# Attention of layers 1 to 3: turned probabilities and values on halves of the array's rows, router and projection matmuls moved behind the values

## The chip, the cores and the metric

One core of a Trainium2 chip. The metric is the device time of one execution, in microseconds (us); the kernel before has a median of 2300.88 us over 3 runs (2300.48 to 2303.32). One further execution was taken by the profiler.

## The reference, cut to what matters

Four layers of gated cross attention, each followed by a feed-forward part, on x of 16 batches x 56 tokens x 256 features. Layer 0 is another kind of attention. In layers 1 to 3 every token has 16 heads, and each batch attends to its own 1500 context rows of 64 numbers, which are the keys and the values at once:

```python
k_r    = einsum('bld,hdr->bhlr', kv_rope, W_kr)
scores = einsum('bhsr,bhlr->bhsl', q_r, k_r)
attn   = softmax(scores, axis=-1)
ctx_c  = einsum('bhsl,bld->bhsd', attn, kv_rope)
out    = (ctx_c through w_kc_kv).reshape(b, s, H * K) @ Wo.T
x      = x + tanh(g_xattn[l]) * out
```

All is float32. The feed-forward parts are mixtures of experts in layers 0, 2 and 3 (a router picks experts token by token) and one matrix with fp8 rounding in layer 1.

## The kernel before, in words

**Tiles and steps.** The 16 batches are taken in 8 tiles of two batches. The weights of the keys are absorbed into the queries, so a query is 64 numbers long; those of a tile's two batches (b = 0 and 1) lie on partitions 0 to 63 and 64 to 127 of `qT`. A tile has 2 x 56 x 16 / 2 = 896 query columns for each batch, cut into nq = 7 steps of QT = 128. So a layer has 56 steps, and layers 1 to 3 have 168. `attention_mla` runs them in a software pipeline: in iteration k, step k gets its scores, step k-1's probabilities are turned, and step k-2's values are made. Every engine's order is the order of the program (`in_order`); the tile framework adds the semaphores.

**One iteration** on the TensorE (PE), in order:

- S, `scores` (L760): six calls, for each third z of the keys and each batch b one of 64 rows x 500 columns. A float32 call is two passes, so this is 12 matmuls. The two batches use different halves of the array's rows and different PSUM banks: `sp0[z]` for b = 0, a third of `sp1` for b = 1.
- V, `values` (L840): 24 calls, each for one of 12 chunks c of 125 keys and one b: 125 rows, 64 columns, 128 moving columns; 48 matmuls, all into one bank, `lent[0]`, taken from the two-bank pool `misc`. The two batches use different halves of the array's columns.
- T, `turned` (L822): 24 transposes of 128 queries x 125 keys in six groups n of 4, one bank per group (n = 1 to 3 use `sp0[n - 1]`, the others `misc`). A transpose is one matmul.

Around them: VectorE (DVE) makes the maxima (L772, L774, L777), copies the groups n = 0 and 1 out of PSUM (L830) and multiplies the values by the inverse denominators in `keep` (L851, two pieces of 64 x 128, or four in the step j = 3, which straddles two column blocks). ScalarE (ACT) makes the exponentials (L783, L792) and copies groups n = 2 to 5 (L832). GpSimd (POOL) adds denominators (L803, L804).

**Other matmuls in the iteration.** When a tile is finished, a generator carries its projection and the next part's preparation on, one piece per iteration at marked slots ("X", "Z", "R", "E"). The pieces with matmuls stand at slot "Z": the projection (L863), and then in layers 2 and 3 three of the router (L1022, L1032, L1073 with L1075), in layer 1 three of the fp8 matrix (L1640, L1662, L1640). Below they are called products. They write into free columns of the bank that holds the values: `room(n)` gives `lent[0][:, QT:QT + n]`. Slot "Z" lies between the second and the third group of transposes. In layer 1 the next tile's keys are also turned (`keys`, L745, three parts of 4 transposes, into a bank of their own), between S and V. In layers 2 and 3 they are loaded instead.

**The loop** that the change reorders, shortened:

```python
if val:
    val.values()
    val.keep()
for i in range(6):
    if new and i == 2:
        new.exps1()
        new.invert()
    if turn:
        turn.turned(i)
    if i == 1:
        ...
        go("Z")
    if turn:
        turn.keep_turned(i)
    if i == 1:
        go("R")
go("E")
```

Of the kernel before, what the change touches and what calls it, by code (L numbers as in the profile page):

```python
# [36 lines left out]
F32 = mybir.dt.float32  # L37
# [4 lines left out]
ALU = mybir.AluOpType  # L42
AX = mybir.AxisListType
# [6 lines left out]
NT = B // 2  # L50
KP, KC = 125, 12
DQ = 192
QT = 128
# [29 lines left out]
def flamingo_kernel(ctx: ExitStack, tc: tile.TileContext, d: dict, out: bass.AP):  # L83
    nc = tc.nc
# [9 lines left out]
    in_order = tc.keep_in_program_order  # L94

    def misc():
        return psm.tile([128, 512], F32, tag="m", name="m_ps")

    lent = [None]

    def room(n):

# [15 lines left out]
    ident = const.tile([128, 128], F32, name="ident")  # L118
    make_identity(nc, ident)
    tri = const.tile([TP, 16, 16], F32, name="tri")  # L120
    kv = const.tile([KP, NT, KC, 2, DC], F32, name="kv")
# [576 lines left out]
    def attention_mla(l, nxt, router=None, behind=None, tail=None):  # L698

        with ExitStack() as st:  # L700
# [3 lines left out]
            def keys_again(t):  # L704

                kvTs[t] = kp.tile([128, L], F32, name="kvT")
                in_order(nc.sync.dma_start(kvTs[t], turned_kv[t]))
# [4 lines left out]
            kvTs = {}  # L712
# [19 lines left out]
            ctxs = {}  # L732
            nq = 8 * TP // QT

            def keys(t, z):

                if l > 1:
                    if z == 0:
                        keys_again(t)
                    return  # L740
                if z == 0:
                    kvTs[t] = kp.tile([128, L], F32, name="kvT")
                ps = misc()
                for c in range(4):
                    in_order(nc.tensor.transpose(  # L745
                        ps[:, c * KP : (c + 1) * KP], kv[:, t, 4 * z + c].rearrange("p b e -> p (b e)"), ident[0:KP, 0:KP]
                    ))
                in_order(nc.scalar.copy(kvTs[t][:, z * 4 * KP : (z + 1) * 4 * KP], ps[:, 0 : 4 * KP]))
                if z == 2:
                    in_order(nc.sync.dma_start(turned_kv[t], kvTs[t]))  # L750

            class Step:
                def __init__(self, t, j):
                    self.t, self.j = t, j

                def scores(self, z):

                    t, j = self.t, self.j
                    for b, o in enumerate((sp0[z], sp1[:, z, :])):
                        in_order(nc.tensor.matmul(  # L760
                            o[:, 0 : 4 * KP],
                            qT[64 * b : 64 * b + 64, t, j * QT : (j + 1) * QT],
                            kvTs[t][64 * b : 64 * b + 64, z * 4 * KP : (z + 1) * 4 * KP],
                            start=True,
                            stop=True,
                        ))

                def maxima0(self, z):
                    if z == 0:
                        self.part = ap.tile([QT, 3], F32, name="part")  # L770
                        self.nm = [ap.tile([QT, 1], F32, name=f"nm{b}") for b in range(2)]
                    in_order(nc.vector.tensor_reduce(self.part[:, z : z + 1], sp0[z][:, 0 : 4 * KP], AX.X, ALU.max))  # L772
                    if z == 2:
                        in_order(nc.vector.tensor_reduce(self.nm[0], self.part, AX.X, ALU.max, negate=True))  # L774

# [3 lines left out]
                def exps0(self):  # L779
                    self.p = [ap.tile([QT, L], F32, name=f"p{b}") for b in range(2)]  # L780
                    self.den = ap.tile([QT, 4], F32, name="den")
                    for z in range(3):
                        in_order(nc.scalar.activation(  # L783
                            self.p[0][:, 4 * z * KP : 4 * (z + 1) * KP],
                            sp0[z][:, 0 : 4 * KP],
                            AF.Exp,
                            bias=self.nm[0],
                            accum_out=self.den[:, z : z + 1],
                        ))
# [20 lines left out]
                    for b in range(2):  # L810
                        in_order(nc.sync.dma_start(self.rep[64 * b : 64 * b + 64, :], through[b : b + 1, :].to_broadcast([64, QT])))

                def turned(self, n):

                    if n == 0:
                        self.pT = ap.tile([KP, KC, 2, QT], F32, name="pT", bufs=1)
                    z, b = n // 2, n % 2
                    ps = sp0[n - 1] if 1 <= n <= 3 else misc()
                    ps = ps[0:KP, :].rearrange("p (c q) -> p c q", c=4)
                    for c in range(4):  # L820
                        k = (4 * z + c) * KP
                        in_order(nc.tensor.transpose(ps[:, c, :], self.p[b][:, k : k + KP], ident))  # L822
                    self.turning = ps

                def keep_turned(self, n):

                    z, b, ps = n // 2, n % 2, self.turning
                    o = self.pT[:, 4 * z : 4 * z + 4, b, :]
                    if n < 2:
                        in_order(nc.vector.tensor_copy(o, ps))  # L830
                    else:
                        in_order(nc.scalar.copy(o, ps))  # L832

                def values(self):

                    lent[0] = misc()
                    self.pv = lent[0][:, 0:QT]
                    for c in range(KC):
                        for b in range(2):
                            in_order(nc.tensor.matmul(  # L840
                                self.pv[64 * b : 64 * b + 64, :], kv[:, self.t, c, b, :], self.pT[:, c, b, :], start=c == 0, stop=c == KC - 1
                            ))

                def keep(self):

                    for a in range(2):
                        lo, hi = max(self.j * QT, 448 * a), min((self.j + 1) * QT, 448 * (a + 1))
                        for b in range(2):
                            if lo < hi:
                                cols = slice(lo - self.j * QT, hi - self.j * QT)  # L850
                                in_order(nc.vector.tensor_tensor(  # L851
                                    ctxs[self.t][64 * a : 64 * a + 64, b, lo - 448 * a : hi - 448 * a],
                                    self.pv[64 * b : 64 * b + 64, cols],
                                    self.rep[64 * b : 64 * b + 64, cols],
                                    ALU.mult,
                                ))

            def project(t):
# [16 lines left out]
            def at(i):  # L875
                return steps[i] if 0 <= i < n else None

            for z in range(3 if l == 1 else 0):
                keys(0, z)
            after, wanted, pending = iter(()), "X", None  # L880

            def go(slot):

                nonlocal wanted
                if wanted[0] == slot:
                    wanted = next(after, "none")

            for k in range(n + 2):
                new, turn, val = at(k), at(k - 1), at(k - 2)
                if k == 1:  # L890

                    for _ in late:
                        pass
                    if l != 2:
                        nxt.stack.close()
                    occupy(10)
                if new:
                    if new.j == 0:
                        ctxs[new.t] = ap.tile([128, 2, H // 2 * S], F32, name="ctxT")
                    for z in range(3):  # L900
                        new.scores(z)
                        new.maxima0(z)
                    if new.t + 1 < NT and new.j in (2, 3, 4):
                        keys(new.t + 1, new.j - 2)
                if k == 0:
                    late = late()
                    next(late, None)
                go("X")
                if new:
                    new.exps0()  # L910
                    new.maxima1()
                if val:
                    val.values()
                    val.keep()
                for i in range(6):
                    if new and i == 2:
                        new.exps1()
                        new.invert()
                    if turn:
                        turn.turned(i)  # L920
                    if i == 1:
                        if pending:
                            for _ in after:
                                pass
                            after, wanted, pending = pending, "Z", None
                        go("Z")
                    if turn:
                        turn.keep_turned(i)
                    if i == 1:
                        go("R")  # L930
                go("E")
                if tail is not None and k > 0:
                    next(behind, None)
                    next(behind, None)
                if val and val.j == nq - 1:
                    pending = project(val.t)
# [917 lines left out]
```

## Time and profile before

| what | us |
|---|---|
| median of 3 runs | 2300.88 (2300.48 to 2303.32) |
| the profiled execution, its own time | 2298.12 |
| its span, first to last instruction | 2296.3 |
| PE busy (share of the span) | 2198.5 (96%) |
| PE weight loads busy | 1598.8 (70%) |
| DVE busy | 1562.3 (68%) |
| ACT busy | 1221.7 (53%) |
| POOL busy | 346.3 (15%) |
| layers' steps, 339 to 844: PE busy of 505.0 | 504.2 |
| layers' steps, 987 to 1484: PE busy of 497.0 | 494.3 |
| layers' steps, 1620 to 2113: PE busy of 493.0 | 487.8 |

The profiler's own time is 1.8 us longer than the span. A line of the timeline gives the start, the length, the engine, the kernel's line and how many instructions are merged in it; two lines of one engine can overlap, because a matmul's recorded length runs on past the start of the next. PEld is the loading of the weights (the stationary operand), which runs beside PE.

### The profile page before, as it was taken

Reading aid. Unit: us, or ns where it says so; the run is one execution under the profiler, and the core shown is the slowest. Engines: PE = TensorE matmul, PEld = TensorE weight load, DVE = VectorE, ACT = ScalarE, POOL = GpSimd, SP = SyncE. Lnnn points to the kernel's source line nnn. Section 1 sums busy time; section 2 is a strip of 40 time slices with the busy share of each in tenths; the row PEclk is TensorE's granted clock in tenths of the full one; section 3 lists DMA queues with packets and bytes.
Section 4 is the critical chain, followed back from the end, with each engine's and each line's share of the span. In section 5 each row is a group of like instructions: output and inputs, shape, how many; then the busy total and the mean of one; then the engine's idle time right before and its main releaser. Section 6 shows DMA issues by size and latency. Waiting matters only on the chain. (4 is left out here: it accounts for less than half of the span.)

```text
span 2296.3 us, 47100 instructions
## 1 busy us (share of the span) xinstructions
PE 2198.5 (96%) x17838; PEld 1598.8 (70%) x17846; DVE 1562.3 (68%) x3627; ACT 1221.7 (53%) x2675; POOL 346.3 (15%) x678
## 2 busy tenths in 40 slices
PE   8879999999999999999999999989999999999698
PEld 5647657777777784457777777745677777777465
DVE  5658457777777878767777777624677777777332
ACT  4313357666666653366666666514666666666132
POOL 1225600000000004410000000000001111101234
PEclk9779999999999999999999999999999999999799
DMA  9545450000000002100000000154001100000465
GB/s 273 183 136 163 141 158 23 22 22 23 16 15 22 23 23 81 57 20 22 25 24 24 25 12 23 49 206 142 20 22 31 30 30 21 27 22 18 135 196 168
DMA packets 106681, 153.48 MB, mean 67 GB/s; under 512 B 18319, under 2 KB 76696, under 8 KB 105417
## 3 DMA queue, kind: packets, MB, share of 16 engines
q1 hardware_dynamic: 97299, 131.83, 18.9%
q0 software_dynamic: 7600, 17.14, 2.3%
q8 instruction: 146, 2.39, 0.4%
q10 hardware_dynamic: 1542, 1.34, 0.2%
q14 instruction: 94, 0.77, 0.1%
HBM read 111.73 MB, written 40.48 MB: 66 GB/s over the span
## 5 line engine op out<-in xcount | busy, mean ns | idle before, releaser
L783 ACT ACTIVATE p<-s_ps,nm 128x500 f32<-128x500 f32 x504 | 335.2, 674 | 402.1 <-DVE nm L774 396.3
L840 PEld LDWEIGHTS m_ps<-pT,kv 125*64 125x64 f32 x8064 | 437.0, 137 | 112.5 <-issue 108.8
L840 PE MATMUL m_ps<-pT,kv 125*64 125x128 f32 x8064 | 478.2, 275 | 3.7 <-ACT pT L832 2.5
L772 DVE TENSOR_REDUCE part<-s_ps 128x1 f32<-128x500 f32 x504 | 341.8, 678 | 203.0 <-PE s_ps L760 200.0
L760 PE MATMUL s_ps<-kvT,qT 64*128 64x500 f32 x2016 | 471.7, 596 | 3.1 <-ACT qT L330 2.6
L760 PEld LDWEIGHTS s_ps<-kvT,qT 64*128 64x128 f32 x2016 | 182.4, 186 | 179.1 <-issue 115.6
L822 PE MATMUL m_ps<-ident,p 128*125 128x128 f32 x2016 | 292.6, 281 | 2.4 <-issue 2.4
L777 DVE TENSOR_REDUCE nm<-s_ps 128x1 f32<-128x1500 f32 x168 | 287.5, 1711 | 0.0
L822 PEld LDWEIGHTS m_ps<-ident,p 128*125 128x125 f32 x2016 | 246.2, 187 | 33.6 <-issue 28.2
L822 PE MATMUL s_ps<-ident,p 128*125 128x128 f32 x2016 | 265.3, 274 | 1.5 <-ACT p L783 1.0
L792 ACT ACTIVATE p<-s_ps,nm 128x1500 f32<-128x1500 f32 x168 | 254.5, 1515 | 4.5 <-DVE nm L777 4.4
L822 PEld LDWEIGHTS s_ps<-ident,p 128*125 128x125 f32 x2016 | 241.9, 188 | 4.0 <-ACT p L783 1.6
L832 ACT COPY pT<-s_ps 125x512 f32<-125x512 f32 x336 | 180.8, 595 | 99.7 <-PE s_ps L822 87.1
L803 POOL TENSOR_TENSOR den<-den 128x1 f32<-128x1 f32 x168 | 32.5, 193 | 1325.9 <-ACT p L783 1325.7
L832 ACT COPY pT<-m_ps 125x512 f32<-125x512 f32 x336 | 185.1, 619 | 0.0
L851 DVE TENSOR_TENSOR ctxT<-m_ps,rep 64x128 f32<-64x128 f32 (+1 forms) x384 | 104.3, 272 | 65.6 <-PE m_ps L840 52.0
L1336 PE MATMUL gu_ps<-wgu,xT 128*128 128x448 f32 (+2 forms) x344 | 138.3, 528 | 4.4 <-ACT xT L1326 4.4
L830 DVE COPY pT<-m_ps 125x512 f32<-125x512 f32 x168 | 116.2, 692 | 10.5 <-PE s_ps L822 0.5
L330 ACT COPY qT<-q_ps 64x224 f32<-64x224 f32 x124 | 69.7, 562 | 98.5 <-PE q_ps L378 67.1
L1361 POOL DMA_INDIRECT results<-y,to x78 | 92.8, 1189 | 169.3 <-ACT y L1360 116.9
L830 DVE COPY pT<-s_ps 125x512 f32<-125x512 f32 x168 | 114.4, 681 | 0.0
L1341 DVE TENSOR_TENSOR act<-gu_ps,act 128x224 f32<-128x224 f32 (+2 forms) x78 | 31.3, 401 | 120.7 <-ACT act L1340 88.8
(305 smaller groups left out, 2518.4 us busy)
## 6 DMA issues: line engine op xcount, KB each, us to landing
rows<-zero SPq DMA_DIRECT2D x16, 899.5 KB
kvT<-turned_kv SPq DMA_DIRECT2D x16, 750.0 KB
rep<-through SPq DMA_DIRECT2D x336, 32.0 KB
xrow<-rows SPq DMA_DIRECT2D x78, 128.5 KB
wgu<-in_L_wgu SPq DMA_DIRECT2D x21, 448.0 KB
wgu<-in_L_wgu SPq DMA_DIRECT2D x8, 1024.0 KB
back<-results SPq DMA_DIRECT2D x16, 448.0 KB
wq<-in_L_wq SPq DMA_DIRECT2D x24, 256.0 KB
```

The source lines that it names most:

```text
L760: in_order(nc.tensor.matmul(o[:, 0 : 4 * KP], qT[64 * b : 64 * b + 64, t, j * QT : (j + 1) * QT], kvTs[t][64 * b : 64 * b + 64, z * 4 * KP ...
L772: in_order(nc.vector.tensor_reduce(self.part[:, z : z + 1], sp0[z][:, 0 : 4 * KP], AX.X, ALU.max))
L777: in_order(nc.vector.tensor_reduce(self.nm[1], sp1[:, :, 0 : 4 * KP], AX.XY, ALU.max, negate=True))
L783: in_order(nc.scalar.activation(self.p[0][:, 4 * z * KP : 4 * (z + 1) * KP], sp0[z][:, 0 : 4 * KP], AF.Exp, bias=self.nm[0], accum_out=sel ...
L792: in_order(nc.scalar.activation(self.p[1].rearrange("p (z c) -> p z c", z=3), sp1[:, :, 0 : 4 * KP], AF.Exp, bias=self.nm[1], accum_out=se ...
L822: in_order(nc.tensor.transpose(ps[:, c, :], self.p[b][:, k : k + KP], ident))
L830: in_order(nc.vector.tensor_copy(o, ps))
L832: in_order(nc.scalar.copy(o, ps))
L840: in_order(nc.tensor.matmul(self.pv[64 * b : 64 * b + 64, :], kv[:, self.t, c, b, :], self.pT[:, c, b, :], start=c == 0, stop=c == KC - 1))
L851: in_order(nc.vector.tensor_tensor(ctxs[self.t][64 * a : 64 * a + 64, b, lo - 448 * a : hi - 448 * a], self.pv[64 * b : 64 * b + 64, cols] ...
L1336: in_order(nc.tensor.matmul(ps[:, s, 0:n], xT[:, k, :], wgu[:, k, s * n : (s + 1) * n], start=k == 0, stop=k == 1))
L1361: i = nc.gpsimd.indirect_dma_start(flat, bass.IndirectOffsetOnAxis(ap=to[:, 0:1], axis=0), y, None, bounds_check=B * S * top - 1, oob_is_e ...
```

## The change

Five things, all in `attention_mla`:

- The transposes work on halves of the rows: a block of 128 queries x 125 keys is two transposes of 64 queries, one on array rows 0 to 63, one on rows 64 to 127, each with 64 moving columns, into two banks. There are 48 of them, in three groups n of 16; each group fills a pair of banks.
- The banks `sp0` rotate: step k's third z lies in `sp0[(k + z) % 3]`. With a, b, c the banks of z = 0, 1, 2 of the new step, group 0 takes (a, b), group 1 (c, a `misc` bank), group 2 (a again, a `misc` bank).
- The values work on halves of the rows: 48 calls, of 64 or 61 rows, 64 columns and 128 moving columns. Rows 0 to 63 of each chunk sum into `lent[0]`, rows 64 to 124 into a second bank, `beside[0]`. `keep` multiplies each part by the inverse denominators on DVE (128 x 128, two of them), and POOL adds the two parts.
- Slots "Z" and "R" now stand right behind V and `keep`, ahead of the transposes.
- Layer 1's keys are turned in four parts of three, in the steps j = 2 to 5, behind slot "Z", into `beside[0]`.

DVE copies both halves of group 0, ACT both halves of groups 1 and 2. The scores are the same matmuls as before. The core of the diff:

```diff
-    lent = [None]
+    lent, beside = [None], [None]
...
-                ps = misc()
-                for c in range(4):
+                ps = (misc() if ps is None else ps[:, QT:])[:, 0 : 3 * KP]
+                for c in range(3):
...
+                def bank(self, z):
+                    return sp0[(nq * self.t + self.j + z) % 3]
...
+                    a, b, c = (sp0[(at + z) % 3] for z in range(3))
+                    pair = (a, b) if n == 0 else (c, misc()) if n == 1 else (a, misc())
+                    self.turning[n] = [ps[0:KP, :].rearrange("p (c b q) -> p c b q", c=4, b=2) for ps in pair]
                     for c in range(4):
-                        k = (4 * z + c) * KP
-                        in_order(nc.tensor.transpose(ps[:, c, :], self.p[b][:, k : k + KP], ident))
+                        for b in range(2):
+                            cut = slice((4 * n + c) * KP, (4 * n + c + 1) * KP)
+                            for h, ps in enumerate(self.turning[n]):
+                                half = slice(64 * h, 64 * h + 64)
+                                in_order(nc.tensor.transpose(ps[:, c, b, :], self.p[b][half, cut], ident[half, half]))
+                def keep_turned(self, n, h):
+                    o = self.pT[:, 4 * n : 4 * n + 4, :, 64 * h : 64 * h + 64]
+                    copy = nc.vector.tensor_copy if n == 0 else nc.scalar.copy
+                    in_order(copy(o, self.turning[n][h]))
...
+                    beside[0] = misc()
                     lent[0] = misc()
-                    self.pv = lent[0][:, 0:QT]
+                    self.pv = [ps[:, 0:QT] for ps in (lent[0], beside[0])]
...
+                            for h, keys_of in enumerate((slice(0, 64), slice(64, KP))):
+                                in_order(nc.tensor.matmul(
+                                    self.pv[h][64 * b : 64 * b + 64, :],
+                                    kv[keys_of, self.t, c, b, :],
+                                    self.pT[keys_of, c, b, :],
...
                 def keep(self):
+                    v = [ap.tile([128, QT], F32, name=f"v{h}") for h in range(2)]
+                    for h in range(2):
+                        in_order(nc.vector.tensor_tensor(v[h], self.pv[h], self.rep, ALU.mult))
...
-                                in_order(nc.vector.tensor_tensor(
+                                in_order(nc.gpsimd.tensor_tensor(
...
+                if pending:
+                    for _ in after:
+                        pass
+                    after, wanted, pending = pending, "Z", None
+                go("Z")
+                if l == 1 and new and new.t + 1 < NT and new.j in (2, 3, 4, 5):
+                    keys(new.t + 1, new.j - 2, beside[0])
+                go("R")
+                if turn:
+                    turn.turned(0, k)
+                    turn.keep_turned(0, 0)
+                    turn.keep_turned(0, 1)
+                if new:
+                    new.exps1()
+                    new.invert()
+                if turn:
+                    turn.turned(1, k)
+                    turn.keep_turned(1, 0)
+                    turn.turned(2, k)
+                    turn.keep_turned(2, 0)
+                    turn.keep_turned(1, 1)
+                    turn.keep_turned(2, 1)
                 go("E")
```

## The prediction

> **What bounds the kernel now.** The page first: PE is busy 96% of the span, at 9 tenths in nearly every slice; ACT and DVE never reach that through the three layers.
>
> ```profile
> PE 2198.5 (96%) x17838; PEld 1598.8 (70%) x17846; DVE 1562.3 (68%) x3627; ACT 1221.7 (53%) x2675; POOL 346.3 (15%) x678
> ...
> PE   8879999999999999999999999989999999999698
> ...
> DVE  5658457777777878767777777624677777777332
> ```
>
> Only PE time counts, so I read PE alone, in order of time, through a plain step and one with keys and a projection (columns: start, length, engine, line, names, shapes, count).
>
> ```profile
> 403.46 2.79 PE L760 MATMUL s_ps<-kvT,qT 64*128 64x500 f32 x12
> 406.17 2.84 PE L840 MATMUL m_ps<-pT,kv 125*64 125x128 f32 x48
> 408.94 0.70 PE L822 MATMUL m_ps<-ident,p 128*125 128x128 f32 x4
> ...
> 411.76 2.79 PE L760 MATMUL s_ps<-kvT,qT 64*128 64x500 f32 x12
> 414.48 0.65 PE L745 MATMUL m_ps<-ident,kv 125*128 125x125 f32 x4
> 415.05 2.84 PE L840 MATMUL m_ps<-pT,kv 125*64 125x128 f32 x48
> ...
> 418.80 3.71 PE L863 MATMUL m_ps<-G,ctxT 128*112 128x256 f32 x16
> ```
>
> A plain step is 411.76 - 403.46 = 8.30 us: S 2.71, V 2.77, T 2.82. How much is streaming? The score loads run in pairs 0.42 apart, so S is 6 x 0.42 = 2.51. V's 48 loads (2.60 us, one 0.137) give (2.60 - 0.14) / 23 = 0.107 to 0.109 a pair: 24 x 0.109 = 2.62. The transposes stand 0.109 apart ((1.39 - 0.19) / 11 below): 24 x 0.109 = 2.62. Sum 7.75. The other 0.55 is three changes of the array's shape, each about 0.09 of draining plus the first load, which nothing covers: 0.10 for 125 or 128 columns, 0.05 for 64. So entering V costs 0.15, entering T 0.20, entering S 0.20.
>
> The rows that decide on the change are these:
>
> ```profile
> 1733.81 0.51 PEld L822 LDWEIGHTS m_ps<-ident,p 128*125 128x125 f32 x4 [0.17 <-issue]
> 1734.24 1.39 PEld L822 LDWEIGHTS s_ps<-ident,p 128*125 128x125 f32 x12
> 1736.63 0.30 PEld L760 LDWEIGHTS s_ps<-kvT,qT 64*128 64x128 f32 x4
> ```
> ```profile
> 1725.01 0.93 DVE L851 TENSOR_TENSOR ctxT<-m_ps,rep 64x64 f32<-64x64 f32 x4 [0.29 <-PE m_ps L840]
> ...
> 1725.99 0.47 PEld L1032 LDWEIGHTS m_ps<-wr,xt 128*112 128x112 f32 x4 [0.15 <-DVE ctxT L851]
> ```
> ```profile
> 902.94 0.92 PE L376 MATMUL q_ps<-r,er 128*128 128x448 f32 x2
> 903.78 0.97 PE L378 MATMUL q_ps<-r,er 128*64 128x448 f32 x4
> ```
>
> **The change, part by part.**
>
> *Transposes on halves: no time.* L1032 moves only 16 columns, yet its four loads of 112 columns take 0.47: (0.47 - 0.19) / 3 = 0.093 each, so a load costs 0.83 ns per column and bounds the pace. For the 125 columns of p that is 0.104, and the four L822 loads in 0.51 give the same ((0.51 - 0.19) / 3). Halving the rows leaves 125 columns. Moving 64 columns takes half of 0.107, but each pair of halves still waits for its 0.104 of loading, if the two loads run side by side: L760's four loads of 64 rows in 0.30 are two rounds of two (one after the other they'd need 3 x 0.107 + 0.19 = 0.51). So 24 pairs at 0.109: 2.62 again. Bounds: 24 x 0.055 (moving alone) to 48 x 0.109 (loads in turn); I take the middle, the row of the same operation.
>
> [...]
>
> *Values on halves: no time.* Four quarters at once, each moving 128 columns: 48 calls x 2 passes x 0.109 / 4 = 2.62. Two row halves at once are seen in L760, two column halves in L840; four aren't. Bounds 2.62 to twice that.
>
> *Row switches.* T and S now have the same shape, so entering S saves 0.20. S to V and V to T still change columns (128, 64, 128). Does that alone cost? L376 to L378 keeps 128 rows and goes to 64 columns: two matmuls at 0.373 should take 0.75 and take 0.84, so 0.09 of draining. They cost as today. Gain 0.20 a step.
>
> *A wait inside T.* Group 2 reuses bank a, where group 0's first half lies until DVE has copied it. Counted from T's first load: eight pairs, the last starts at 0.10 + 7 x 0.109 = 0.86, its record ends 0.27 later, DVE starts 0.05 after (V ends 1733.88 by its record, L851 starts 1733.93), the copy takes 0.68 (L830), PE's load 0.05 more: 1.9. PE wants that load at 0.10 + 15 x 0.109 = 1.74. Stall 0.15, bounds 0 and 0.2. Before, groups 4 and 5 used banks long free. Bank c (exponentials over before T starts) and the `misc` bank of group 1 (second multiplication over at T + 0.78, wanted at T + 0.87) just hold. Group 0's second copy ends at 2.6, S wants its bank at 2.75.
>
> A plain step is then 8.30 - 0.20 + 0.15 = 8.25; over 168 steps -8 us.
>
> *Products behind V: the cost.* They write the bank that holds the values, and L1032 above shows that the framework makes such a write wait for the reads of pv, though the columns differ: L851 ends 1725.94, the load starts 1725.99. Today four transposes or eight stand in between, which hide it except where the values are those of step j = 3, in four pieces. Behind V nothing does. L851 starts 0.12 after T starts today; one multiplication of 128 columns 0.29 (L851); semaphore 0.05: the product starts 0.46 after V's drain. Then the product (128 rows) to T (64 rows) is a further change: about 0.19. So +0.65, less what it waits already: about 0.60 for 63 products and 0.45 for the 21 of step j = 3. Their number: 4 a tile, 7 tiles in the loop, 3 layers: 84. 63 x 0.60 + 21 x 0.45 = +47 us. Bound below: no wait, 84 x 0.19 = 16; above: both multiplications waited for, +0.3 each, 72.
>
> *Keys.* Before: 414.48 to 415.05 is 0.58 x 21 = 12. After, 28 parts into `beside`, whose multiplication is the second: in the steps j = 3 and 4 a wait of 0.12 + 0.61 + 0.05 = 0.78, three transposes 0.32, change 0.19, so 1.29 each; behind a product (j = 2 and 5, counted by the step with scores) 0.33. (2 x 1.29 + 2 x 0.33) x 7 = 23. +11.
>
> *DVE, POOL, SP.* Two multiplications of 0.29 replace two to four of 0.22 to 0.29: nothing. POOL's adds of 64 x 128: between 0.19 (L803, one column) and 1.13 (L370, 448 columns), so 0.46 each by their slope, on an engine that is 15% busy. Queued behind them are the denominator additions, about 0.9 late; their inverse goes through SP's four small DMAs and is wanted more than a step later. If that cover were gone it would show as DVE waiting at L851. DVE's "X" pieces (0.4 to 0.75) delay `keep` where they fall; left in the range.
>
> **Sum:** -8 + 47 + 11 = +50 us. The profiled execution had 2298.1 (span 2296.3 and 1.8 around it): 2348. The median of the runs is 2.8 above it: 2300.9 + 50 = **2350**.
>
> **Rivals.**
>
> 1. *Faster: changes of columns are free while the rows stay.* Then S to V and V to T lose 0.15 and 0.20 too: 0.35 x 168 = 59 less, **2291**. Against: L376 to L378, 0.09 at equal rows. For: no row shows it at 64. It decides if V's last matmul to T's first is under 0.12 in a plain step. Chance 0.15.
> 2. *The halves load in half the time:* T falls by 24 x (0.109 - 0.056) = 1.27, x 168 = 214: **2137**. Against: L760's loads of 64 rows last as long as those of 128 (0.187 to 0.188). Chance 0.04.
> 3. *No wait behind V* (the change does only what it says): -84 x 0.46 and -14 x 0.78: **2301**. Against: L1032's and L1640's waits for L851. Chance 0.10.
> 4. *PE can't issue so fast.* V's 192 instructions in 2.62 are 13.6 ns each. Densest rows: V today, 96 in 2.62 (27 ns), and L596 in layer 0, 32 loads and 32 matmuls with 1.01 from the first load to the last (16 ns, and held by the loading of its 64 columns, 0.053 a pair). At 16: 3.1, +0.5 a step, 2436. At 27: 5.2, +2.6 a step, 2785, less what is queued ahead when V begins. Chance 0.14, nearer to the lower end, since L596's pace has another cause.
>
> [...]
>
> **How the numbers follow.** Forecast 0.57, rivals 0.15, 0.04, 0.10, 0.14. A measurement of this kernel can tell 0.2% from no change, 4.6 us. Faster: rivals 1 and 2, 0.19. Same: most of rival 3, 0.08. Slower 0.73. The forecast's own bounds: stall 0 and products 16: about 2297 at the least; upper bound of the products 2375. The range from 2285 to 2395 takes in forecast and rivals 1 and 3, with some room for the X pieces, and leaves out 2 and 4, 0.18.
>
> **What would show it.** In the profile after: plain steps at 8.2 to 8.3; T to S without a gap; 24 pairs of transposes 0.109 apart, with a hole of some 0.15 before group 2; a wait of PE for DVE's multiplication ahead of every product; keys' steps at 9.5. Wrong if T is near 1.4, if V is over 2.9, if a product's load starts with V's last matmul, or if a gap between V and T is gone.

## The result and the profile after

The kernel after takes 2421.8 us (median of 4 runs, 2418.1 to 2435.9); the kernel before took 2301.5 beside it (4 runs). The ratio is 1.0533, with a 95% interval from 1.049 to 1.0576: 120 us slower, where the prediction had 49. The profiled execution took 2423.0 us, 124.9 more than that of before.

First the page of after: the engines, and the clock that was granted to PE in 40 slices (tenths of full speed); the last line is the clock of before.

```profile
PE 2258.5 (93%) x29942; PEld 1630.2 (67%) x29942; DVE 1529.5 (63%) x3579; ACT 1250.0 (52%) x2683; POOL 507.2 (21%) x1062
...
PEclk9779999999999999999999999989999989999799
```
```profile
PEclk9779999999999999999999999999999999999799
```

PE was busy 96% of the span and is busy 93%, with 12,100 matmuls more. Something now leaves PE idle. Next a plain step of after, the answer to the rows at 403.46 of before (start, length, engine, line, names, shapes, count).

```profile
1073.95 2.73 PE L760 MATMUL s_ps<-kvT,qT 64*128 64x500 f32 x12
1076.62 2.85 PE L844 MATMUL m_ps<-pT,kv 64*64 64x128 f32 x96
1079.40 1.19 PE L826 MATMUL s_ps<-ident,p 64*125 64x64 f32 x17
...
1082.26 2.73 PE L760 MATMUL s_ps<-kvT,qT 64*128 64x500 f32 x12
```
```profile
1079.52 0.49 DVE L856 TENSOR_TENSOR v<-m_ps,rep 128x128 f32<-128x128 f32 x2 [0.30 <-PE m_ps L844]
1080.59 1.29 DVE L832 COPY pT<-s_ps 125x512 f32<-125x512 f32 x2 [0.58 <-PE s_ps L826]
```

The step is 1082.26 - 1073.95 = 8.31, within 0.01 as long as before. By the starts of its matmuls, V lasts 2.58 from its first to its last (before 2.57), V to T takes 0.199 (0.203), T lasts 2.75 (2.61) and T to S takes 0.106 (0.202). T's pairs stand 0.109 apart, but group 2 waits for DVE's first copy: its first load starts 0.243 after the last matmul of group 1, where other pairs' loads start 0.053 after one. What the common shape of T and S gives, some 0.15 (0.10 in the gap, 0.05 at the first scores), the wait takes back.

The list of waits, longest in total first, names what PE waits for in the kernel after (us in total, times, longest).

```profile
PE m_ps L741 <- DVE v L856: 13.4, 16, 1.2
PE m_ps L874 <- DVE v L856: 10.3, 21, 0.5
...
PE m_ps L844 <- issue: 7.9, 14, 1.0
PE m_ps L844 <- ACT pT L832: 7.0, 6, 1.2
```

L856 is the multiplication of the values. Products and keys wait for it as foretold. "Issue" in the middle of the values is another thing: nothing is waited for that the profile shows.

I then set each of the 165 steps beside the same step of before. Most differ by one of a few exact amounts: 0.00 a plain step, +0.73 one with a projection, +0.60, +0.34 and +0.51 the router's, +0.55 and +1.20 the keys. The rest are longer by odd amounts, and nearly all of these overlap a stretch of half clock. The stretches of the layers' steps show it (before, then after: length, then busy time and count of PE, PEld, DVE, ACT and POOL, then the mean granted clock, DMA share, GB/s).

```profile
338.00:834.20 496.20, 495.79 (x4750) 382.35 (x4750) 391.01 (x866) 319.31 (x682) 21.23 (x110) 1.00 0.06 21
986.80:1474.30 487.50, 485.26 (x4677) 374.52 (x4677) 366.55 (x811) 306.50 (x665) 31.81 (x135) 1.00 0.07 21
1618.70:2111.70 493.00, 487.82 (x4680) 376.11 (x4681) 373.46 (x818) 313.60 (x686) 57.05 (x160) 1.00 0.09 25
```
```profile
340.90:871.40 530.50, 504.81 (x8591) 385.06 (x8590) 379.89 (x850) 327.85 (x688) 72.20 (x232) 0.99 0.06 21
1029.70:1537.40 507.70, 492.45 (x8517) 378.29 (x8517) 356.44 (x795) 314.87 (x663) 82.92 (x257) 0.99 0.08 22
1692.90:2225.80 532.90, 511.67 (x8521) 389.54 (x8521) 363.41 (x802) 321.63 (x684) 107.80 (x282) 0.96 0.08 24
```

Before, the clock is 1.00 in all three. After, 61 us of the steps run at half clock, 41 of them in layer 3; in the whole execution it is 198.5 us instead of 109.5. So 28 of the added 89 us lie outside the layers' steps. I take half clock to lose half its length (in one such stretch the score loads stand 0.84 apart, at full clock 0.42), which is too much wherever PE waits anyway. The added time, taken apart, is therefore an estimate:

| part | us |
|---|---|
| products (+44.8) and keys (+12.8), priced by steps at full clock | +57.6 |
| plain steps | 0.0 |
| holes in the values of layer 3, 6 x (11.04 - 8.30), priced by the one of these steps that has no half clock, less the 5.8 of before | +10.6 |
| 61.4 us more at half clock within the steps, halved | +30.7 |
| 27.6 us more at half clock outside them, halved | +13.8 |
| the rest, by difference: among it the second step of each layer, and what stands behind the layers' last steps | +12.2 |
| profiled execution, 2423.0 - 2298.1 | +124.9 |

**When the clock drops.** The stretches of half clock are 3.41 us long or multiples of it, and all begin on one grid of 3.413 us. So I cut the trace along the grid and worked out, from the starts and moving columns of all matmuls (0.83 ns a column, as L760's 500 in 0.42; half of that in bfloat16, as L133's 512 in 0.216), in which share of each window the array streams. Within the layers' steps of after, 13 windows at full clock were followed by one at half; their shares are 0.26 to 0.414. The other 429 were not; their lowest share is 0.416. In the kernel before the lowest of 432 is 0.54. Here is one drop, in four windows of the grid (columns as above).

```profile
1818.60:1822.00 3.40, 3.31 (x100) 2.73 (x97) 3.14 (x7) 1.88 (x5) 0.24 (x1) 1.00 0.09 24
1822.00:1825.40 3.40, 2.75 (x47) 2.54 (x46) 2.40 (x8) 2.40 (x5) 1.29 (x4) 1.00 0.00 0
1825.40:1828.80 3.40, 3.40 (x16) 1.81 (x16) 1.89 (x8) 1.56 (x3) 1.84 (x2) 0.50 0.14 37
1828.80:1832.20 3.40, 2.68 (x50) 1.60 (x47) 2.79 (x4) 1.18 (x3) 2.02 (x3) 0.99 0.36 106
```

In the second window PE waits until 1822.65 for VectorE (0.74 in the timeline, ahead of L1090) and then transposes. "2.75 busy" hides what the array does: 23 pairs that stream 0.053 each are 1.22 us, and with L1090 and the end of the values the array streams for 0.38 of the window. The next runs at 0.50. On 128 rows 23 transposes would stream 23 x 0.107 = 2.46, so by this estimate the same wait would have left a share of over 0.7.

PE is idle in the second window for 0.63 us at the longest, and in none of the 13 for more than 0.98. In the kernel after, the share of streaming tells the windows apart, with the edge between 0.414 and 0.416. Experiment 7 shows what this measure lacks.

### The profile page after: what moved, and what is told of

It is laid out like the page before. It is cut to its first block, busy times and chain, and to the rows that moved or that the text cites. A ratio compares the mean times of both kernels' runs of the same rounds, so it can differ in the third digit from the quotient of the medians.

```text
span 2421.2 us, 72195 instructions
## 1 busy us (share of the span) xinstructions
PE 2258.5 (93%) x29942; PEld 1630.2 (67%) x29942; DVE 1529.5 (63%) x3579; ACT 1250.0 (52%) x2683; POOL 507.2 (21%) x1062
## 5 line engine op out<-in xcount | busy, mean ns | idle before, releaser
L844 PEld LDWEIGHTS m_ps<-pT,kv 64*64 64x64 f32 (+1 forms) x16128 | 448.0, 134 | 141.1 <-issue 119.1
L826 PE MATMUL s_ps<-ident,p 64*125 64x64 f32 x5376 | 516.3, 276 | 4.0 <-ACT p L783 4.0
L844 PE MATMUL m_ps<-pT,kv 64*64 64x128 f32 (+1 forms) x16128 | 494.0, 274 | 15.2 <-issue 7.9
L826 PEld LDWEIGHTS s_ps<-ident,p 64*125 64x125 f32 x5376 | 473.2, 188 | 50.9 <-issue 20.7
L760 PE MATMUL s_ps<-kvT,qT 64*128 64x500 f32 x2016 | 483.8, 610 | 3.1 <-ACT qT L330 2.6
L862 POOL TENSOR_TENSOR ctxT<-v,v 64x128 f32<-64x128 f32 (+1 forms) x384 | 160.6, 418 | 1249.6 <-DVE v L856 1235.6
L826 PE MATMUL m_ps<-ident,p 64*125 64x64 f32 x2688 | 359.8, 277 | 0.0
L826 PEld LDWEIGHTS m_ps<-ident,p 64*125 64x125 f32 x2688 | 326.4, 190 | 0.1
L760 PEld LDWEIGHTS s_ps<-kvT,qT 64*128 64x128 f32 x2016 | 191.7, 196 | 170.9 <-issue 122.9
L832 DVE COPY pT<-s_ps 125x512 f32<-125x512 f32 x336 | 216.5, 686 | 132.5 <-PE s_ps L826 131.8
L856 DVE TENSOR_TENSOR v<-m_ps,rep 128x128 f32<-128x128 f32 x336 | 81.9, 286 | 67.9 <-PE m_ps L844 67.9
L874 PE MATMUL m_ps<-G,ctxT 128*112 128x256 f32 x384 | 93.1, 397 | 14.3 <-DVE v L856 10.3
```

Of the source, the lines that this page charges most:

```text
L760: in_order(nc.tensor.matmul(o[:, 0 : 4 * KP], qT[64 * b : 64 * b + 64, t, j * QT : (j + 1) * QT], kvTs[t][64 * b : 64 * b + 64, z * 4 * KP ...
L826: in_order(nc.tensor.transpose(ps[:, c, b, :], self.p[b][half, cut], ident[half, half]))
L832: in_order(copy(o, self.turning[n][h]))
L844: in_order(nc.tensor.matmul(self.pv[h][64 * b : 64 * b + 64, :], kv[keys_of, self.t, c, b, :], self.pT[keys_of, c, b, :], start=c == 0, st ...
L862: in_order(nc.gpsimd.tensor_tensor(ctxs[self.t][64 * a : 64 * a + 64, b, lo - 448 * a : hi - 448 * a], v[0][64 * b : 64 * b + 64, cols], v ...
L874: in_order(nc.tensor.matmul(ps[0:TP, 0:D], ctxT.rearrange("p b (s h) -> p h (b s)", s=S)[:, h, :], G[:, h, :], start=h == 0, stop=h == H / ...
```

## Theories

**C**: the half clock comes from halving the transposes. Their pace stays, but the array streams only half of the time (0.053 of each 0.109), so that any further wait in the same window brings it under some 0.41. **W**, the rival: the new waits behind the values bring it down, whatever T's shape. **F**, on the holes: PE's instructions come late while the scattered row transfers of layer 3 occupy the transfer engines; its rival **G**: GpSimd's own order delays something that the values need. Each ratio below is against the kernel before on the same chip.

## Experiment 1: transposes on all rows

```diff
-for h, ps in enumerate(self.turning[n]):
-    in_order(nc.tensor.transpose(ps[:, c, b, :], self.p[b][half, cut], ident[half, half]))
+in_order(nc.tensor.transpose(self.turning[n][b][:, c, :], self.p[b][:, cut], ident))
```

> The kernel after, but each transposition again on all 128 rows of the array (24 of them, one bank for each batch in place of one for each half of the queries); values still on quarters, products still behind the values. Theory C: about 45 us of the change are lost because the granted clock drops to a half for stretches of 3.41 us or multiples of it, and it drops because halved transpositions stream only 0.053 of each 0.109 us, so that any further wait brings a window of 3.41 us under some 0.41 of streaming. Then half clock within the steps of layers 1 to 3 falls from 61 us to under 15, while the change of rows between T and S comes back (0.15 x 168 = +25 us): about 2400 us (2385 to 2412). Theory W (rival): the waits behind the values alone bring the clock down, whatever T's shape: half clock stays at 60 us or so and the time rises by 25 to about 2447 (over 2435).

Measured: 2396.4 us, ratio 1.0403 (1.0379 to 1.0426). Half clock within the steps: 0.9 us. The same view of its three stretches:

```profile
341.50:866.70 525.20, 499.53 (x7292) 385.32 (x7292) 381.15 (x850) 325.61 (x688) 71.86 (x232) 1.00 0.06 21
1024.20:1530.90 506.70, 491.84 (x7222) 378.31 (x7221) 356.20 (x795) 314.55 (x664) 82.58 (x257) 1.00 0.07 21
1687.10:2209.40 522.30, 496.92 (x7224) 380.88 (x7225) 363.30 (x802) 321.26 (x685) 107.37 (x282) 1.00 0.08 25
```

The products still wait behind the values (+0.56 to +0.68 in most of their steps), a plain step costs 0.14 more, and yet the kernel is faster than after. C holds, W falls: the waits are there and the clock stays. The lowest share in a window of the steps is 0.445. The quartered values, still in, do not disturb the clock. Outside the layers' steps, though, half clock stays at 140 us (after 137, before 109.5); in experiment 6, which differs from the kernel after in layer 3 alone, it is 110. So these 28 us do not go with the transposes' shape, and no run tells their cause.

## Experiment 2: products back among the transposes

```diff
-go("Z"); keys(...); go("R"); turn.turned(0, k); turn.keep_turned(0, 0); turn.keep_turned(0, 1)
+keys(...); turn.turned(0, k); go("Z"); turn.keep_turned(0, 0); go("R"); turn.keep_turned(0, 1)
```

> The kernel after, but with the router's and the projection's matmuls between the first and the second group of transposes; the keys of layer 1 stay behind the values, all the rest as after. Both theories: the waits for VectorE ahead of 84 products go (about 45 us of undisturbed extra time, less some 8 for 84 x 0.09 of the change of shape that is left in T). Theory C: the windows with a product lose their idle time, so half clock within the steps falls from 61 us to some 25 (the first steps of each layer keep theirs): about 2365 us (2350 to 2380). If the clock had nothing to do with the waits behind the values, only the 40 us go: about 2382 or more.

Measured: 2400.3 us, ratio 1.0425 (1.0401 to 1.0449); 35 slower than expected. The products did what was expected: the projection +0.15 instead of +0.73, the router's +0.37, -0.13 and -0.04 in most steps of layer 2, +0.37, +0.09 and -0.23 in layer 3 (they fill T's wait for DVE's copy). The half clock within the steps did not: 57 us, where some 25 were expected. The keys' waits (+1.3 us a step where a product follows), the first steps of the layers and the holes of layer 3 bring it down as well: with halved transposes the products' wait is not the only one that does. Behind two of the six holes the step took 14.1 us, 5 more than before.

## Experiment 3: streaming in the place of waiting

```diff
+if val and (pending or wanted[0] == "Z" or <keys follow>):
+    for _ in range(3):
+        in_order(nc.tensor.matmul(sp0[k % 3], onesb[:, 0:128], onesb, start=True, stop=True))
 go("Z")
```

> The kernel after with three matmuls of ones (bfloat16, 512 columns, 0.21 us each) put between the values and whatever follows them at that place (product or keys), into a bank that the transposes overwrite next. They run while PE would wait for VectorE (0.46 to 0.8 us). Theory C: each such window gets 0.64 us more of streaming, so it stays over 0.41 of 3.41 us; half clock within the steps falls from 61 us to about 20 to 25 (only the first steps of each layer), for at most 0.1 to 0.2 us more in each of the 105 places: about 2405 us (2392 to 2418). If the clock does not follow the share of time in which the array streams, half clock stays at 60 us and the time rises by 10 to 20: 2432 to 2445.

Measured: 2406.3 us, ratio 1.0453 (1.0418 to 1.0488), as theory C has it: three useless matmuls in each of these steps make the kernel 0.8% faster. Half clock within the steps is 17.1 us, all of it in the first steps of the layers; the three windows ahead of it have shares of 0.29 to 0.34, all others 0.42 or more. A router's step goes from +0.60 to +0.74, so the matmuls are paid for in part.

## Experiment 4: the order alone, in the kernel before

```diff
 val.keep()
+go("Z"); go("R")
 for i in range(6):
-    if i == 1: go("Z") ... go("R")
```

> The kernel before with one part of the change alone: the router's and the projection's matmuls stand behind the values instead of between the second and the third group of transposes. Transposes on 128 rows, values on 125 rows, keys as before. The prediction's price is 63 x 0.60 + 21 x 0.45 = +47 us. Theory C: with transposes on all rows no window in the steps falls under 0.41, so no half clock within the steps: 2348 us (2335 to 2355). Theory W: the waits alone bring the clock down as in the kernel after: some 25 to 40 us more, 2372 to 2390.

Measured: 2367.1 us, ratio 1.0273 (1.0248 to 1.0297): between the two expectations. No product's step lost its clock (the only 6.8 us of half clock within the steps are in the first step of layer 2, behind a window of 0.505, which doesn't fit an edge near 0.41; see experiment 7). So W falls again. The price of a product was wrong: +0.67 to +0.87 in place of 0.60 and 0.45.

```profile
PE m_ps L863 <- DVE ctxT L851: 19.4, 23, 3.7
PE m_ps L1071 <- DVE ctxT L851: 14.4, 14, 1.2
```

In the kernel before both multiplications, or all four, read the bank into which the product writes, so it waits for the last: 0.98 from V's last matmul to most of the products, 1.30 with four pieces. In the kernel after the second reads another bank, and the gap is 0.66 to 0.76 at most of them. This is the prediction's upper bound (72), come true in the other kernel.

## Experiment 5: values on all rows

```diff
-for h, keys_of in enumerate((slice(0, 64), slice(64, KP))):
-    matmul(self.pv[h][64*b : 64*b+64, :], kv[keys_of, t, c, b, :], self.pT[keys_of, c, b, :])
+matmul(self.pv[64*b : 64*b+64, :], kv[:, t, c, b, :], self.pT[:, c, b, :])
...
-in_order(nc.gpsimd.tensor_tensor(ctxs..., v[0]..., v[1]..., ALU.add))
+in_order(nc.vector.tensor_tensor(ctxs..., self.pv..., self.rep..., ALU.mult))
```

> The kernel after with the values as before: 48 matmuls on 125 rows into one bank, two halves of the columns side by side, VectorE multiplying straight into the result and no additions on GpSimd. Transposes on halves and products behind the values as after; the second bank stays for the keys, which no longer wait for a multiplication. If quartering the values costs no array time, plain steps stay at 8.30 us. A product now waits for both multiplications (0.29 each) instead of the first: +0.2 to 0.3 x 84 = about +20; the keys lose their wait, about -10; if the holes in the values of layer 3 come from late instructions, they shrink with 96 instructions in place of 192, -5 to -10; what stands behind the last step of a layer loses GpSimd's additions, 0 to -15. Theory C (halved transposes plus waits bring the clock down): half clock within the steps stays at 45 us or more, time about 2415 us (2395 to 2435). If the quartered values were the cause of the clock's drops, half clock goes to under 15 us and the time under 2390.

Measured: 2439.5 us, ratio 1.0602 (1.0575 to 1.063), slower than expected. Plain steps stay at 8.30, so four quarters at once are worth exactly two halves. The products wait for all multiplications (+0.96 in most steps, +0.34 to +0.73 in the kernel after), and the longer wait drops the clock more often: 95 us of half clock within the steps in place of 61. Longer waits, more half clock: theory C again, now as a dose. The holes of layer 3 shrink to 1.0 us a tile, with 96 instructions in the values instead of 192.

## Experiments 6, 9, 11 and 12: the holes in layer 3

The weight loads of one such step in the kernel after:

```profile
1897.98 1.35 PEld L844 LDWEIGHTS m_ps<-pT,kv 64*64 64x64 f32 x45 [0.74 <-issue]
1900.56 0.21 PEld L844 LDWEIGHTS m_ps<-pT,kv 64*64 64x64 f32 x4 [1.23 <-issue]
1902.00 1.33 PEld L844 LDWEIGHTS m_ps<-pT,kv 64*64 64x64 f32 x47 [1.22 <-issue]
```

Two stops of 1.2 us, released by nothing. They occur only in the step behind the four scattered transfers of a tile. Here a fetch of 16 KB on the instruction queue (q8) falls into them, but in four of the six such steps none does. Instructions are fetched more often after:

```profile
q8 instruction: 146, 2.39, 0.4%
```
```profile
q8 instruction: 241, 3.95, 0.7%
```

The first line is of before, the second of after (packets, MB, share). Experiment 6 takes the kernel after, 9 and 12 the kernel before, with the same line:

```diff
 for j in range(top):
+    if j == 2:
+        yield "E"
     i = nc.gpsimd.indirect_dma_start(...)
```

> The kernel after with one line more: of the four scattered row transfers that GpSimd issues for a tile in layer 3, the last two are issued one step later. In the kernel after the step behind them has three holes in the values' matmuls, 2.7 us in all in each of 6 tiles, in which PE waits for no semaphore. Theory F: PE's instructions come late because their transfer queues behind the scattered rows. Two transfers at a time then hold them up for less than half as long: the two steps together lose at most 1.5 us in place of 2.7, so 6 x 1.2 = about 7 us less, and with the half clock that follows some holes 5 to 10 more: 2405 to 2417 us. Rival G: it is GpSimd's own order that delays something the values need (the additions standing behind four transfers of 1.2 us); then the holes also shrink, but end with the transfers and leave a wait for GpSimd in the list of waits. If neither, the holes stay: 2422 +- 5 us.

Measured: 2413.8 us, ratio 1.0492 (1.0474 to 1.051). The steps behind the transfers take 9.59 to 9.86 in place of 10.78 and more, the steps after them show no holes, and what is left is still "issue". The transfers cause the holes, and GpSimd's order doesn't (G falls). That it is the instructions that come late (F) fits the missing release and experiment 5, but no view shows a fetch waiting, and four of the six steps have no fetch in their stops: it is not shown.

> The kernel before with the line that halved the holes in the kernel after: of a tile's four scattered row transfers in layer 3, the last two are issued one step later. In the kernel before the step behind them is 0.7 to 1.5 us longer than a plain one in 6 tiles, 5.7 us in all. Theory F: with two transfers at a time the instructions come in time again and most of it goes: -3 to -5 us, 2296 to 2298 beside 2301. Rival: the holes are only shared out over two steps: 2301, no difference.

Measured: 2285.2 us, ratio 1.0001 (0.9991 to 1.001). No step behind transfers was longer than 8.30 us, and nothing was gained. But on this chip the kernel before took 2284.5 and not 2301, so I profiled it beside a second try on another chip.

> The kernel before, unchanged, for its profile on the chip on which the next run is made. The run with the transfers in pairs had plain steps of 8.30 us behind the transfers of all tiles and yet the time of the kernel before, which was itself 17 us faster there than on the chips of the other runs. If that chip holds up instructions less, the kernel before has steps of 8.3 us there too; where it takes 2301 us, its steps behind the transfers should be 0.7 to 1.5 us longer, as in its first profile.

> The kernel before with the last two of a tile's four scattered transfers one step later, a second time. Theory F: the step behind the transfers falls to 8.30 us, and where the kernel before loses 5.7 us there the time falls by 3 to 5 us; where it loses nothing, by nothing. Rival: the holes are shared out over two steps, and the time stays, with holes in both.

Measured: the kernel before 2304.8 us in the profiled execution (2302.7 in the median of 11 others), with steps of 8.92 to 9.68 behind the transfers; with the line 2296.8 us (2292.2 to 2298.3), ratio 0.9968 (0.9955 to 0.998), those steps 8.30 to 8.38. Weight loads of one of them, first without the line, then with it:

```profile
1880.26 2.62 PEld L840 LDWEIGHTS m_ps<-pT,kv 125*64 125x64 f32 x47 [0.74 <-issue]
1884.15 0.13 PEld L840 LDWEIGHTS m_ps<-pT,kv 125*64 125x64 f32 x1 [1.27 <-issue]
```
```profile
1878.13 2.68 PEld L840 LDWEIGHTS m_ps<-pT,kv 125*64 125x64 f32 x48 [0.74 <-issue]
```

This is the one version that beats both kernels, by 0.3%, where the holes exist. Whether the kernel before has them on the chip of experiment 9 was not profiled.

## Experiment 7: what sets the pace of the transposes

```diff
-transpose(ps[:, c, b, :], self.p[b][half, cut], ident[half, half])
+transpose(ps[0:64, c, b, :], self.p[b][half, cut][:, 0:64], ident[half, half])
```

> Leaves work out: of each chunk of 125 keys only the first 64 are turned and enter the values (48 matmuls on 64 rows), so a transposition on half of the array's rows loads 64 columns in place of 125 and moves 64 as after. Theory L: the pace of the halved transposes, 0.109 us a pair, is set by loading 125 columns (0.104): then pairs stand 0.055 to 0.06 us apart and T falls from 2.75 to about 1.5 us and the stall before the third group grows, since VectorE's copy doesn't get faster. Rival I: it is set by something that counts instructions or moves (issue, PSUM): pairs stay 0.109 apart. The time itself says nothing of the change.

The kernel leaves out 61 of each 125 keys, in the transposes and in the values. Transposes in the kernel after, then in this one (one of each pair):

```profile
1080.54 0.27 PE L826 MATMUL s_ps<-ident,p 64*125 64x64 f32 x1
1080.65 0.27 PE L826 MATMUL s_ps<-ident,p 64*125 64x64 f32 x1
```
```profile
1063.35 0.22 PE L826 MATMUL s_ps<-ident,p 64*64 64x64 f32 x1
1063.41 0.22 PE L826 MATMUL s_ps<-ident,p 64*64 64x64 f32 x1
...
1064.13 0.24 PE L826 MATMUL s_ps<-ident,p 64*64 64x64 f32 x1 [0.39 <-DVE pT L832]
```

0.054 apart instead of 0.109: theory L. The pace is that of loading, 0.84 and 0.87 ns a column (0.054 for 64, 0.109 for 125), and halving the rows did not change it (0.109 before and after). The last line shows T's wait for DVE's copy, grown as PE got ahead.

This trace also says more of the clock. It has 116 us of half clock within the layers' steps, behind 33 windows of the grid in which the array streams for 0.34 to 0.74 of the time, 32 of them over 0.41. One of them is the second here (columns as above):

```profile
1437.10:1440.50 3.40, 3.40 (x30) 1.64 (x32) 2.26 (x6) 2.21 (x6) 0.00 (x0) 1.00 0.00 0
1440.50:1443.90 3.40, 2.69 (x48) 2.45 (x47) 2.99 (x5) 2.48 (x7) 0.39 (x2) 1.00 0.07 19
1443.90:1447.30 3.40, 3.40 (x8) 2.58 (x9) 0.00 (x0) 1.09 (x2) 0.00 (x0) 0.51 0.00 0
```

The array streams for 0.74 of this window, but nearly all of it are values on 64 of the 128 rows, and then the clock drops. So here the time alone does not tell the windows apart. Count each matmul by the share of the 128 rows that it uses (the two column halves of the values share their rows and count once), and this window comes to 0.37. By that count all 89 drops within the layers' steps of the fourteen profiled runs follow windows of at most 0.386, the one of experiment 4 included (0.385). Of some 6,000 windows without a drop behind them 16 are that low, and none is under 0.363. By time alone 34 of the 89 drops lie above 0.414. Halved transposes in pairs use all rows, for half of the time, so in the kernel after the two counts hardly differ (its highest drop is at 0.386 in place of 0.414). The count was found in these traces afterwards; no run was made to test it.

## Experiment 8: the kernel before with its products one group later

```diff
-if i == 1: go("Z") ... go("R")
+if i == 2: go("Z") ... go("R")
```

> The kernel before with the products one group of transposes later (behind the third in place of the second), nothing else. The prediction read that in the kernel before the multiplications of the values hold up the products only where they come in four pieces (21 of 84). If so, 0.43 us more of cover takes away 0.2 to 0.4 us there: 21 x 0.3 = -6 us, 2295 us beside 2301. Rival: the fifth group reuses the bank of the values, and now only the fourth stands between it and the product, so it waits for VectorE's reading of the product: 84 x 0.1 to 0.3 = 8 to 25 us slower, 2309 to 2326.

Measured: 2329.2 us, ratio 1.0115 (1.0097 to 1.0134): the rival's side, a little beyond. The router's second product (L1032), whose values come in four pieces, gets +0.11 and not -0.3, the projection 0.00, and the other short products about +0.5. The list of waits has a new entry, T waiting for VectorE's reading of a product:

```profile
PE m_ps L822 <- DVE place L1078: 3.9, 12, 0.4
```

Of the places tried in the kernel before, the one between the second and third group is the one that covers both waits on that bank, for the multiplications ahead of the product and for its reading behind it.

## Experiment 10: three repairs at once

Experiment 3, the line of experiment 6, and this:

```diff
+if k == 1:
+    occupy(6)
```

> The kernel after with three things that leave its halves, quarters and order as they are: the three matmuls of ones behind the values (2406 us alone), the four scattered transfers of a tile in two pairs (8 us less alone), and six matmuls of ones (0.21 us each) ahead of the transposes in the second step of a layer, where PE waits 1.56 us for the exponentials and the clock drops next. Theory C: half clock within the steps of layers 1 to 3 falls to under 7 us, from 61 in the kernel after and 17 with the first thing alone, which is worth 5 us more: 2406 - 8 - 6 = about 2391 us (2382 to 2400). If the drop in the first steps has another cause, half clock there stays at 17 us and the time at 2396 to 2404.

Measured: 2375.3 us, ratio 1.0384 (1.0368 to 1.04). Against the 2301 us that the expectation was made for, the ratio gives 2390. Half clock within the steps is 3.4 us. On this chip (that of experiment 9) no holes are left, so the share of that line can't be read here. What remains is the order of the work: 84 products and the keys behind the values, with the matmuls of ones, and about 25 us behind the layers' last steps, of which half clock is a part; I did not take these further apart.

## Why the prediction was wrong

- **Bound.** Right: only PE's time counted, and the plain steps were read to 0.05.
- **Transposes on halves, "no time".** The pace was right (24 pairs, 0.109; experiment 7 shows loading sets it). The step that failed is the conclusion. Equal pace with half the moving columns halves the share of time in which the array streams (0.053 of each 0.109), and in this trace the clock dropped behind windows with a share of 0.414 or less. No term and no rival of the prediction has the granted clock in it, though the page of before has a row for it; 44.5 us went unseen there. Experiment 1 puts the 30.7 within the layers' steps down to this (0.9 us of half clock in place of 61); the other 13.8 have no known cause.
- **Values on halves, "no time".** Right: 2.58 for 2.57, and experiment 5. So rival 4 falls: 192 instructions go at 13.6 ns each for a whole stage, again and again.
- **Row switches.** T to S saved about 0.15, not 0.20: about half of the first load stays uncovered (it starts at 1082.20, its matmul 0.056 later; 0.106 for its 128 columns at 0.83 ns, an estimate). Changes of columns alone cost as before (0.199), so rival 1 falls; rival 2 fell with 0.109.
- **Wait inside T.** 0.15 predicted, 0.14 measured. Together 0.00 a step in place of -0.05: -8 us became 0.
- **Products.** +47 predicted, +44.8 measured at full clock; the gap from V to the product 0.66 to 0.76 (0.80 to 1.01 at the router's third), by the bank that multiplication and product share. The steps differ by 0.34 to 0.73 where 0.45 and 0.60 were predicted, so that the sum is nearer than its parts is luck. Rival 3 falls.
- **Keys.** +11 predicted, +12.8 measured.
- **"X pieces ... left in the range".** Layer 3's steps behind the scattered transfers are longer by 1.8 us a tile than before, 10.6 in all, but not by VectorE: PE stands still there without a release, by the scattered transfers (experiment 6), and for longer with twice the instructions (experiment 5). How the transfers hold it up stays open. Those steps of 9.0 to 9.8 us were in the trace of before and I did not ask what ended them.
- **Sum.** Terms of 50 that came to 57.6, and three that were not there: clock 44.5, holes 10.6, and 12.2 left over, at the beginnings and ends of the layers among others. With the whole clock term the 57.6 make 2403 us, past the range; with only its 30.7 they make 2389, still inside, and the holes carry it out (2400).

## What to carry to other kernels

In this kernel a wait of TensorE had two prices: its length, and, with the transposes on halves, what it left of streaming, and on how many rows, in its 3.413 us of the grid. One stretch of 3.41 us at half clock costs up to 1.7 us (an estimate, half its length), more than twice the wait of 0.74 us (ahead of L1090) that stood before one. So look at the granted clock before a form of an operation with equal pace but less streaming is called free: with transposes on halves of the rows 61 us of the layers' steps ran at half clock, without them 0.9 (experiment 1). If the waits can't go, some matmuls of ones in their place may pay, as here, by 0.8% (experiment 3). Before a product is moved, look at both waits on its PSUM bank, for the last reader ahead of it and for its own reader behind it, and at the work that covers each.

## What the runs showed of the hardware

- Half clock began and ended on a grid of 3.413 us. In the 442 windows of it within the layers' steps of the kernel after, the clock dropped behind a share of streaming of 0.414 or less, and never behind 0.416 or more; PE was idle for at most 0.98 us at a stretch in the windows ahead of the drops. Over all runs the time alone does not tell the windows apart (drops at up to 0.74 with half of the rows in use); the share weighted by rows in use nearly does: all 89 drops at 0.386 or less, 16 of some 6,000 other windows as low.
- Four matmuls of float32 of 64 (or 61) rows and 64 columns ran side by side: 96 of them, of 128 moving columns, took 2.58 us from the first start to the last, and 48 on 125 rows, in pairs, 2.57. Loads and matmuls together went at 13.6 ns an instruction through 192 in a row.
- The transposes' pace was that of loading their columns: 0.109 us for 125, with 64 or 128 columns moved; 0.054 for 64, with 64 moved.
- Four scattered transfers of rows held up TensorE for 0.3 to 1.5 us at 96 instructions in the values (experiment 8 has the lowest) and 2.7 us at 192, without a semaphore; in pairs, one step apart, for 0.0 to 0.1 and 1.3 to 1.6. On the chip of experiments 9 and 10 the pairs left nothing at 192 either.
- The kernel before took 2284.5 us on one chip and 2301 to 2305 on the others.
